# Local attention: the second and third head of every second list swap the engines that evacuate their banks

## The chip, the cores and the metric

The kernel runs on one core of a Trainium2 chip. The metric is the device time of one execution in microseconds (us). A NeuronCore has TensorE (PE in the profile; PEld is its weight load), VectorE (DVE), ScalarE (ACT), GpSimd (POOL) and SyncE (SP), each with an instruction queue of its own, worked off in order; they wait for each other through semaphores. Matmuls write to PSUM banks, of which ScalarE and VectorE bring the results to SBUF.

## The reference, cut to what matters

The program is a two-layer hybrid on an image of 256 channels and 64 x 64 pixels. The change lies in layer 0, a linear attention over boxes around each pixel, with 8 heads of 32 channels and three window sizes:

```python
q = sigmoid(Wq x);  k = sigmoid(Wk x);  v = Wv x / |Wv x|      # x: group-normalised, per head 32 x 64 x 64
Ik, Ikv = integral(k), integral(k outer v)                     # integral images
for w in (1, 2, 4):                                            # boxes of 64, 32 and 16 pixels a side
    attn = einsum('bdhw,bdfhw->bfhw', q, box(Ikv))             # for each pixel: sum of (q.k) v over its box
    norm = einsum('bdhw,bdhw->bhw', q, box(Ik))
    outs.append(attn / (norm + 1e-6))
x = x + Wout(concat(outs)) + bout
```

Layer 1 follows on the 4096 pixels as tokens: causal attention, its feed-forward part, a mixture of experts with two experts chosen, and layer norms. It isn't touched.

## The kernel before

`window_attention` does layer 0 in two head groups of four heads each (`hg` 0 and 1), through `window_heads`. A box sum is split into a part of whole blocks of 8 x 8 pixels, which is taken from block sums (`inside`), and rims. For the rims the kernel forms explicit scores between a tile of 128 keys and a patch of queries, with a mask: a bias of 0 inside the box and -64 outside is added by a matmul with a small table, and a maximum with 0 then wipes what lies outside, since all q and k are positive.

The patches (`Part`) are packed into lists of at most 512 columns, one PSUM bank for each head. In each head group there are 49 vertical lists (`beside`, columns of blocks) and then 108 horizontal ones (`above`, rows of blocks), together 157; `push` handles one list:

1. it takes four psum buffers, one for each head, from a pool of six (`ps`, `bufs=6`), which are handed out in turn;
2. L351: one bias matmul for each part and head, with the heads innermost; the four heads lie on different rows of the TensorE array (32 partitions each) and run side by side;
3. L360: one score matmul for each part and head, q against the keys, in the same banks;
4. `evacuate` (L326 to L330), once for each head in the order 0, 1, 2, 3: maximum with 0 from PSUM to the tile `pm`, by ScalarE (L328) or by VectorE (L330), as a counter says;
5. `add` of the list before: L393, the products of its `pm` with v (tiles `v` or `vh`), summed in accumulators `acc` from a second PSUM pool of two.

The counter runs on over the lists of a head group and is set to 0 at its start. So the dealing repeats after eight evacuations, which is two lists.

TensorE, GpSimd, VectorE and ScalarE run in the order of the program text in this part (`manual_schedule`). On TensorE that gives: bias and scores of list n, products of list n - 1, bias and scores of list n + 1, and so on. A buffer that a list takes must have been evacuated by the engine that holds it. Since four of six buffers belong to the list before, the new list's first two heads get buffers that have been free for long, its third and fourth those of heads 0 and 1 of the list before. Other steps between the lists take buffers from the same pool and shift this: `norms` (`sum_up` L468, `spread_out` L478), `convolve` (L507) and the first steps of layer 1 (`turn`, L887).

Between the lists VectorE and ScalarE do other work: ScalarE copies finished vertical accumulators out (`store`, L404) and sends them to DRAM; VectorE multiplies or adds finished rows (`finish`, L424, L427), takes reciprocals of the norms in four pieces (`invert`, L473), builds block sums (`inner`, L492 to L500) and adds the output projection to the tokens (L512). GpSimd forms the boxes of k (`boxes`, L443 to L456) and multiplies by the reciprocal norms (L428). The raw image for the second head group is loaded into the pool that also holds `pm` (`load`, L190) and normalised (L612).

Of the kernel before, what the change touches and what calls it, by code (L numbers as in the profile page):

```python
# [296 lines left out]
def window_heads(tc, a, t, ident, hg, norm, raws, load, psum, pools, tables, consts, late, causal):  # L297
# [25 lines left out]
    counter = [0]  # L323

    def evacuate(dst, src):
        counter[0] += 1  # L326
        if counter[0] % 8 in (1, 3, 5, 6, 0):
            nc.scalar.activation(dst, src, AF.Relu)  # L328
        else:
            nc.vector.tensor_scalar_max(dst, src, 0.0)  # L330
# [9 lines left out]
    def push(parts):  # L340
# [25 lines left out]
        for h in range(4):  # L366
            evacuate(pm[:, h, 0:at], got[h][:, 0:at])
# [1150 lines left out]
```

## Time and profile before

| | |
|---|---|
| median of 3 runs | 1851.17 us (1850.91 to 1852.68) |
| the profiled execution | 1852.58 us, span 1850.9 us |
| mean granted TensorE clock | 0.986 of full speed |
| TensorE busy over the span | 1773.5 us (96%) |
| VectorE busy | 1017.3 us (55%) |
| ScalarE busy | 834.2 us (45%) |
| GpSimd busy | 510.7 us (28%) |

How to read it: a busy time is the union of an engine's instructions. TensorE's matmuls are pipelined and their ends are modelled, so that a busy TensorE need not be one that gets on. In a line of the timeline stand the start, the duration, the engine, the source line and the operation of instructions that were merged; "out<-in" names the tiles, "x4" is their number, and the bracket tells how long the engine idled before and what ended that. In a line of groups the last part gives busy time and mean duration in ns, then the idle time before and what ended it. The lists of the change run from 75 to 945 us of the span.

### The profile page before, as it was taken

The numbers are of one execution on the slowest core, as the hardware profiler recorded it, in microseconds if no ns is written. First come the engines' busy times: TensorE is split into PE (matmuls) and PEld (weight loads), VectorE is DVE, ScalarE is ACT, GpSimd is POOL, SyncE is SP. The second block draws the span as 40 slices with busy tenths as digits, with TensorE's granted clock in tenths as the row PEclk, the third lists the DMA queues.
The fourth block names the chain that finished last, engine by engine and source line by source line (L and its number), as shares of the span: only waits on it lengthen the run. The fifth ranks groups of instructions, "written<-read, shape, count | busy, mean of one in ns | idle before, by whom it ended". The sixth has DMA issues, their size and how long they took to land.

```text
span 1850.9 us, 41533 instructions
## 1 busy us (share of the span) xinstructions
PE 1773.5 (96%) x17740; PEld 1203.0 (65%) x17740; DVE 1017.3 (55%) x2068; ACT 834.2 (45%) x1588; POOL 510.7 (28%) x767
## 2 busy tenths in 40 slices
PE   6999999999899999999999999999999999699998
PEld 4654555555465455555568888878778777478777
DVE  6544556666464566677663345554565565634333
ACT  3566444444356655545422334544444544432232
POOL 2484223342147123333212022022012112032110
PEclk9999999999999999999999999999999999799999
DMA  5331100000231110000200000000000000010000
GB/s 179 115 99 59 30 14 19 14 19 13 91 108 42 42 30 14 19 13 18 55 2 1 0 1 1 1 1 1 1 1 1 1 1 1 7 51 12 23 23 23
DMA packets 66617, 53.03 MB, mean 29 GB/s; under 512 B 37312, under 2 KB 56536, under 8 KB 66432
## 3 DMA queue, kind: packets, MB, share of 16 engines
q1 hardware_dynamic: 52688, 27.67, 5.5%
q10 hardware_dynamic: 12480, 18.87, 3.0%
q0 software_dynamic: 1264, 3.84, 0.8%
q8 instruction: 139, 2.28, 0.5%
q14 instruction: 46, 0.38, 0.1%
HBM read 32.93 MB, written 17.44 MB: 27 GB/s over the span
## 4 chain that ended last, share of the span: by engine, by line
PE 44%; DVE 5%; ACT 2%; issue 1%; POOL 0%; ACTq 0%; DVEq 0%; POOLq 0%
PE pa L1042 10%; PE po L1115 10%; PE ph L1452 6%; PE py L1472 6%; PE pm L971 1%; PE pm L1176 1%; PE pm L1185 1%; PE acc L393 1%; PE ps L507 1%; DVE lnst L735 1%; PE ps L360 1%; DVE max L1058 1%; PE pm L899 1%; ACT s L1054 1%; DVE s L1093 1%
## 5 line engine op out<-in xcount | busy, mean ns | idle before, releaser
L328 ACT ACTIVATE pm<-ps 128x448 f32<-128x448 f32 (+12 forms) x784 | 368.5, 534 | 326.3 <-issue 174.1
L330 DVE TENSOR_SCALAR pm<-ps 128x448 f32<-128x448 f32 (+15 forms) x472 | 272.3, 605 | 255.6 <-PE ps L360 161.5
L360 PE MATMUL ps<-q,kh 32*128 32x248 f32 (+14 forms) x2688 | 213.5, 397 | 0.0
L393 PE MATMUL acc<-pm,vh 128*32 128x248 f32 (+14 forms) x2688 | 201.4, 401 | 0.0
L1042 PE MATMUL pa<-qT,k 128*128 128x256 f32 (+1 forms) x800 | 184.9, 375 | 0.0
L1058 DVE TENSOR_TENSOR max<-max,pa 128x512 f32<-128x512 f32 x105 | 71.7, 683 | 189.8 <-ACT s L1054 189.7
L351 PE MATMUL ps<-table,table 32*128 32x192 bf16 (+9 forms) x1984 | 158.3, 284 | 8.5 <-ACT pm L328 5.7
L1094 ACT ACTIVATE s<-s 128x512 f32<-128x512 f32 x136 | 85.5, 630 | 178.5 <-DVE s L1093 174.8
L1042 PEld LDWEIGHTS pa<-qT,k 128*128 128x128 f32 x800 | 150.2, 190 | 23.6 <-issue 2.2
L351 PEld LDWEIGHTS <-table 32*128 32x128 bf16 x1984 | 51.3, 91 | 166.3 <-issue 160.6
L428 POOL TENSOR_TENSOR y<-y,rn 128x512 f32<-128x512 f32 x32 | 41.0, 1281 | 416.6 <-DVE y L427 364.3
L360 PEld LDWEIGHTS ps<-q,kh 32*128 32x128 f32 x2688 | 125.2, 184 | 8.1 <-issue 4.9
L393 PEld LDWEIGHTS acc<-pm,vh 128*32 128x32 f32 x2688 | 64.8, 108 | 90.2 <-issue 72.6
L1054 ACT COPY s<-pa 128x512 f32<-128x512 f32 x120 | 69.9, 582 | 115.1 <-PE pa L1042 115.0
L1472 PE MATMUL py<-w,hT 128*128 128x256 f32 x512 | 111.8, 379 | 0.0
L1115 PE MATMUL po<-kh,s 128*128 128x257 f32 x406 | 105.6, 388 | 2.5 <-ACT s L1094 2.5
L1472 PEld LDWEIGHTS py<-w,hT 128*128 128x128 f32 x512 | 97.3, 190 | 15.7 <-issue 1.9
L360 PE MATMUL ps<-q,k 32*128 32x448 f32 (+5 forms) x1280 | 99.1, 403 | 0.0
L393 PE MATMUL acc<-pm,v 128*32 128x448 f32 (+5 forms) x1280 | 96.4, 409 | 0.0
L1093 DVE TENSOR_TENSOR s<-s,tops 128x512 f32<-128x512 f32 x136 | 95.2, 704 | 1.0 <-ACT tops L1086 1.0
L507 PE MATMUL ps<-l0wo,y 128*128 128x256 f32 x384 | 90.7, 387 | 0.0
L1115 PE MATMUL po<-v,s 128*128 128x257 f32 x342 | 86.9, 385 | 1.8 <-ACT s L1094 1.8
(320 smaller groups left out, 2890.4 us busy)
## 6 DMA issues: line engine op xcount, KB each, us to landing
oscratch<-ov ACTq DMA_DIRECT2D x32, 256.0 KB
ov<-oscratch SPq DMA_DIRECT2D x32, 256.0 KB
vscratch<-v SPq DMA_DIRECT2D x32, 128.0 KB
vh<-vscratch SPq DMA_DIRECT2D x16, 256.0 KB
t<-in_xT ACTq DMA_DIRECT2D x16, 256.0 KB
raw<-in_x ACTq DMA_DIRECT2D x7, 512.0 KB
raw<-in_x SPq DMA_DIRECT2D x7, 512.0 KB
out<-y SPq DMA_DIRECT2D x7, 512.0 KB
```

Of the source, the lines that this page charges most:

```text
L328: nc.scalar.activation(dst, src, AF.Relu)
L330: nc.vector.tensor_scalar_max(dst, src, 0.0)
L351: nc.tensor.matmul(got[h][:, spot].rearrange("p (y x) -> p y x", y=part.r1 - part.r0), lhsT=spread[hs, int(part.vertical), :], rhs=bias[hs ...
L360: nc.tensor.matmul(got[h][:, spot].rearrange("p (y x) -> p y x", y=part.r1 - part.r0), lhsT=keys[hs], rhs=q[hs, part.r0 : part.r1, part.c0 ...
L393: nc.tensor.matmul(out, lhsT=v, rhs=pm[:, h, spot].rearrange("p (y x) -> p y x", y=part.r1 - part.r0), start=fresh, stop=(left[key] == 0), ...
L507: nc.tensor.matmul(pt[:, i * D : (i + 1) * D], lhsT=ys[wi, Y][:, (2 * j + i) * P : (2 * j + i + 1) * P], rhs=wo[:, n, :], start=(n == 0), ...
L1042: nc.tensor.matmul(pp[:, k * 2 * P + at : (k + 1) * 2 * P], lhsT=key, rhs=qT[:, c, q0 + at : q0 + 2 * P], start=(c == 0), stop=(c == DC - 1))
L1058: nc.vector.tensor_tensor(u["max"], old, pp, op=ALU.max)
L1093: nc.vector.tensor_tensor(s, s, u["top"].unsqueeze(1).to_broadcast([P, 2, 2 * P]), op=ALU.subtract)
L1115: nc.tensor.matmul(acc, lhsT=u[b][:, (2 * k + j) * P : (2 * k + j + 1) * P], rhs=v[2 * b + k][:, 0 : D + 1], start=(b == h and k == 0), st ...
L1452: nc.tensor.matmul(ph, lhsT=w1v[:, e, c, f, :], rhs=x2[g][c], start=(c == 0), stop=(c == DC - 1))
L1472: nc.tensor.matmul(py, lhsT=hT[:, e, f, j * P : (j + 1) * P], rhs=w2v[:, e, f, :], start=(e + f == 0), stop=(e == 1 and f == FC - 1))
```

## The change

`evacuate` sends the count modulo 8 to ScalarE where it is in a set, and to VectorE otherwise. One member of the set changes:

```diff
     def evacuate(dst, src):
         counter[0] += 1
-        if counter[0] % 8 in (1, 3, 5, 6, 0):
+        if counter[0] % 8 in (1, 3, 5, 7, 0):
             nc.scalar.activation(dst, src, AF.Relu)
         else:
             nc.vector.tensor_scalar_max(dst, src, 0.0)
```

| | head 0 | head 1 | head 2 | head 3 |
|---|---|---|---|---|
| even lists, before and after | ScalarE | VectorE | ScalarE | VectorE |
| odd lists, before | ScalarE | ScalarE | VectorE | ScalarE |
| odd lists, after | ScalarE | VectorE | ScalarE | ScalarE |

Lists are numbered from 0 in each head group, so 78 of the 157 are odd.

## The prediction

> **What bounds the kernel now.** I read the totals of the page first, then the busy time in four stretches (the two passes over the vertical lists, 75 to 190 and 538 to 652 us, and the two over the horizontal lists, 190 to 476 and 652 to 945 us), then the waits, then the costliest groups, and last the timeline around single lists.
>
> ```profile
> PE 1773.5 (96%) x17740; PEld 1203.0 (65%) x17740; DVE 1017.3 (55%) x2068; ACT 834.2 (45%) x1588; POOL 510.7 (28%) x767
> ```
> ```profile
> 190.00:476.00 286.00, 283.42 (x4572) 154.46 (x4567) 174.03 (x288) 136.39 (x289) 89.12 (x103) 1.00 0.07 17
> 652.00:945.00 293.00, 290.38 (x4619) 159.45 (x4611) 202.62 (x391) 144.78 (x309) 88.61 (x99) 1.00 0.09 22
> ```
> The columns of the stretches are PE, PEld, DVE, ACT and POOL busy, the granted clock, the DMA share and GB/s. TensorE is marked busy 99% of both stretches at full clock; VectorE is busy 61 to 69%, ScalarE about 48%, GpSimd 30%. So TensorE's own queue sets the end of this stage, and only time inside that queue can be won.
>
> ```profile
> PE ps L351 <- ACT pm L328: 5.7, 28, 0.2
> ```
> ```profile
> L328 ACT ACTIVATE pm<-ps 128x448 f32<-128x448 f32 (+12 forms) x784 | 368.5, 534 | 326.3 <-issue 174.1
> L330 DVE TENSOR_SCALAR pm<-ps 128x448 f32<-128x448 f32 (+15 forms) x472 | 272.3, 605 | 255.6 <-PE ps L360 161.5
> ```
> In the waits of the first 1000 us, TensorE is idle for ScalarE's evacuations for 5.7 us only, 28 times. That figure is too small: it counts a gap only where the modelled end of the matmul before has passed. The timeline shows the rest. Here are two lists in a row with one part of the same shape each (448 columns); lines of other engines are left out:
>
> ```profile
> 154.88 1.51 ACT L328 ACTIVATE pm<-ps 128x488 f32<-128x488 f32 x3 [1.27 <-PE ps L360]
> 155.03 0.67 DVE L330 TENSOR_SCALAR pm<-ps 128x488 f32<-128x488 f32 x1 [1.17 <-issue]
> ...
> 155.53 0.79 PE L351 MATMUL ps<-table,table 32*128 32x448 bf16 x4
> ...
> 155.98 1.09 PE L360 MATMUL ps<-q,k 32*128 32x448 f32 x8
> ...
> 157.00 1.03 PE L393 MATMUL acc<-pm,v 128*32 128x168 f32 x16
> 157.08 0.98 ACT L328 ACTIVATE pm<-ps 128x448 f32<-128x448 f32 x2 [0.69 <-ACT pm L328]
> 157.13 1.16 DVE L330 TENSOR_SCALAR pm<-ps 128x448 f32<-128x448 f32 x2 [1.44 <-PE ps L360]
> ...
> 157.97 0.37 PE L351 MATMUL ps<-table,table 32*128 32x448 bf16 x4
> ...
> 158.17 0.92 PE L360 MATMUL ps<-q,k 32*128 32x448 f32 x8
> 159.02 0.96 PE L393 MATMUL acc<-pm,v 128*32 128x448 f32 x8
> ```
> At 155.53 us four bias matmuls, one per head, should start within 0.01 us of each other and run side by side. Instruction by instruction, three do; the fourth starts at 155.98, 0.05 us after ScalarE's second evacuation of the list before ended. From first bias matmul to first product this list takes 157.00 - 155.53 = 1.47 us; the next one, behind a list dealt two and two, takes 159.02 - 157.97 = 1.05 us. TensorE lost 0.42 us and the page called it busy.
>
> **The change part by part.** Six psum buffers serve four heads. List n+1 normally gets the two free buffers and then the banks of heads 0 and 1 of list n, so its third and fourth bias matmuls wait for those two evacuations. In an odd list (0 based) ScalarE now takes heads 0, 1 and 3 and VectorE head 2; afterwards ScalarE takes 0, 2, 3 and VectorE 1. Even lists stay. Nothing is added or removed: ScalarE keeps 784 evacuations, VectorE 472, with the same shapes. In the built order only TensorE's waits differ: at L351, 156 move from ScalarE to VectorE and 46 the other way; at L393, 110 move from VectorE to ScalarE.
>
> What the bank of head 1 gains: over the 156 odd lists ScalarE's second evacuation starts a median 0.44 us after its first and takes 0.54; VectorE's single one starts 0.11 us after ScalarE's first and takes 0.62. VectorE ends a median 0.25 us sooner, though in 19 lists later, where it is busy with something else. The Trainium skill (ScalarE: Activation LUTs, Step-by-step) says "ScalarE is closer to PSUM, VectorE is closer to SBUF"; by that alone a bank handed to VectorE would come free later. The rows agree on the length, 0.62 against 0.54 us, but the bank no longer stands second in a queue, which is worth more.
>
> For the sum I took each list's four bias matmuls one by one, replaced the end of the awaited evacuation by that of the engine that will do it (VectorE's single evacuation and ScalarE's second keep their times and swap banks), and let a matmul start 0.051 us after it, as 191 waits of the trace do. From first to fourth bias matmul, summed:
> - 93 odd lists whose successor takes the banks as above: 24.9 us now, 8.7 afterwards, 16.2 won.
> - 17 whose successor has a ScalarE or VectorE wait further ahead, but where again only the fourth moves: 6.8 now, 3.2 afterwards, 3.6 won.
> - 46 where other work took buffers between (convolve, spread_out, turn), so that the successor needs heads 1 and 2 both: 6.3 us either way; 0.03 won, called nothing.
> The sum is 19.9 us, half in each head group (10.3 and 9.6), over 110 waits.
>
> Does TensorE's queue give this back? Among the one-part 448-column lists (40 of them), a fourth matmul that is 0.01, 0.23 and 0.44 us behind the first gives 1.050, 1.255 and 1.470 us to the first product. Over 18 shapes it is the same: what is lost is the stall less some 0.014 us, since the other three heads absorb that much. So 40 stalls that vanish give back 40 x 0.014 = 0.6 us less. Replaying the stage with every engine's order and durations moves 0.2 us more, where a faster TensorE meets a late VectorE. Net 19.9 - 0.6 - 0.2 = 19.1 us.
>
> The other new waits: products of head 2 now wait for ScalarE's second evacuation, but they start after the next list's scores, one microsecond or so after it. The bank of head 2 comes free 0.25 us later; it goes to the list after next as its first buffer, behind a whole list's products. Behind the fourth bias matmul stands all of TensorE's queue, so a late VectorE costs in full; the two lists where it would (at 324.7 and 751.1 us, 0.06 and 0.24 us later) are in the sum. GpSimd and the DMAs move with TensorE. GpSimd waits 50.8 us in two places for L468 in the vertical passes, so 4.5 us won in each does not bring it onto the path.
>
> The profiled execution took 1852.58 us (span 1850.9), 1.4 above the median of 1851.17. 1852.58 - 19.1 = 1833.5; against the median **1832.1 us**.
>
> **Rivals.**
> - *Only the idle time counts.* If the merged rows are right that TensorE waits 5.7 us, no more than that comes: 1851.2 - 5.7 = 1845.5. Against it stand the pairs of equal lists. 5%.
> - *The stage ends elsewhere.* If GpSimd's boxes or the loads between the head groups set the end, the gain is swallowed: about 1851. For it: TensorE does wait for loads near 476 to 483 us. Against: those loads start when TensorE's products free the buffers, so they move along. 5%.
> - *VectorE late, slower.* The bank of head 1 leaves an engine that always comes at once for one that is 61 to 69% busy. In the horizontal lists VectorE also has 64 reciprocals of 0.94 us (L473) and 31 adds of 0.69 (L427). If those now stood ahead of head 1 in the odd half of the lists, each costs its length less the 0.25 us margin: 32 x 0.69 + 15 x 0.44 = 28.7 us, so 28.7 - 19.1 = 9.6 us slower, 1860.8. It decides where VectorE's start is late by more than 0.25 us on average; today VectorE is the later of the two in 8 of the 110 waits that count, and in six of these TensorE comes later than both. 3%.
> - *The clock falls otherwise.* Behind the stage the granted clock is 0.62 over 10.2 us (from 1574.4) and 0.56 over 20.4 us (from 1608.6). Moved forward by 19 us, TensorE's idle stretches there may meet one such drop more or less; one of the size of the first is 0.38 x 10.2 = 3.9 us: 1836.0, or 1828.2. The Trainium skill (TensorE: Matmul & The Clock Gate, What's actually happening) says that the activity window is free-running, about 3.4 us long, so that the drop depends on where in it the work lands. The windows here are of such lengths, but the three runs of before lie within 1.8 us, so it seldom matters. 7%, half each way.
>
> **How the numbers follow.** My forecast, TensorE passing on nearly all of the 19.1 us, has 80%: 1832.1, give or take 4 for the other engines' interplay. The range 1828 to 1840 holds this case and most of the clock's; the idle-only rival, the swallowed gain and the slower case stay outside, 13% in all. A measurement of this kernel can tell about 0.2%, 3.7 us, from no change. Faster is 80 + 7 + 5 = 92%, same 5%, slower 3%.
>
> **What would show it.** Right: in the changed profile the fourth bias matmul behind odd lists follows VectorE's single evacuation; the L351 waits for L328 fall well below 5.7 us, some waits for L330 appear in their place; the list whose bias matmuls start at 155.53 us takes about 1.24 us to its first product where it took 1.47; the last L393 product of the stage ends some 19 us sooner, half of it in each head group; from there on all stands as before but earlier. Wrong: L351 waiting long for L330 with L473 or L427 ahead of it; a stage that ends as late as before with TensorE idle for L612, L446 or a load; or the stage 19 us shorter and the time behind it longer, at a lower clock.

## The result, and the profile after

| | before | after |
|---|---|---|
| median | 1851.71 us (6 runs, 1850.91 to 1852.80) | 1834.01 us (6 runs, 1832.68 to 1836.38) |
| profiled execution | 1852.58 us, span 1850.9 | 1832.68 us, span 1831.0 |
| span's start to the first L351 | 75.3 us | 73.8 us |
| first to last L351, first head group | 397.9 us | 388.8 us |
| from there to the second head group's first L351 | 65.6 us | 65.8 us |
| first to last L351, second head group | 403.2 us | 393.8 us |
| from there to the end | 909.0 us | 908.7 us |

The ratio is 0.9905, 95% interval 0.9892 to 0.9917: faster by 17.7 us, where 19.1 were forecast and 1832.1 us predicted. The profiled execution of after happens to be the fastest of its six. The last five rows, read from the trace of the profiled execution, say where the time came from: 9.1 and 9.4 us out of the two runs of lists, 18.2 us with what lies between; behind them 0.3 us. The 1.4 us at the start are not the change's: over all the kernels with an unchanged start that point lies between 73.8 and 75.3 us.

The totals of the page after:

```profile
PE 1759.7 (96%) x17740; PEld 1198.3 (65%) x17740; DVE 1008.5 (55%) x2068; ACT 833.9 (46%) x1588; POOL 512.4 (28%) x767
```
The instruction counts are the same, and ScalarE's busy time is within 0.3 us of what it was. TensorE's "busy" time fell by 13.8 us although it executes the same matmuls: most of what was won had been counted as work.

The groups of the page and the waits of TensorE over the first 1000 us, after:

```profile
L328 ACT ACTIVATE pm<-ps 128x448 f32<-128x448 f32 (+12 forms) x784 | 368.5, 535 | 308.7 <-issue 173.9
L330 DVE TENSOR_SCALAR pm<-ps 128x448 f32<-128x448 f32 (+15 forms) x472 | 272.0, 604 | 238.0 <-PE ps L360 151.5
```
```profile
PE ps L351 <- ACT pm L328: 1.3, 4, 0.3
...
PE ps L351 <- DVE pm L330: 0.6, 3, 0.2
```
An evacuation costs what it did (534 and 605 ns before). The idle time for ScalarE went from 5.7 to 1.3 us, and 0.6 us for VectorE appeared. The view shows 3.8 us of change where the stage took 18.2 us less.

The timeline of after around the two equal lists of the prediction (lines of other engines and of weight loads left out):

```profile
152.28 1.51 ACT L328 ACTIVATE pm<-ps 128x488 f32<-128x488 f32 x3 [1.21 <-PE ps L360]
152.38 0.67 DVE L330 TENSOR_SCALAR pm<-ps 128x488 f32<-128x488 f32 x1 [1.08 <-issue]
152.94 0.51 PE L351 MATMUL ps<-table,table 32*128 32x448 bf16 x4
153.14 1.06 PE L360 MATMUL ps<-q,k 32*128 32x448 f32 x8
154.13 1.03 PE L393 MATMUL acc<-pm,v 128*32 128x168 f32 x16
...
155.09 0.37 PE L351 MATMUL ps<-table,table 32*128 32x448 bf16 x4
...
156.14 0.96 PE L393 MATMUL acc<-pm,v 128*32 128x448 f32 x8
```
The three evacuations of ScalarE take 1.51 us as before, VectorE's one 0.67. But the fourth bias matmul now waits only for VectorE, until 152.38 + 0.67 = 153.05 us, and not for ScalarE's second evacuation; instruction by instruction it starts at 153.10. The four are spread over less time (L351 x4 lasts 0.51 us, 0.79 before), and the first product comes 154.13 - 152.94 = 1.19 us after the first bias matmul, where it was 1.47 (1.24 was forecast). The list after it takes 1.05 us as before: nothing was there to be won.

### The profile page after: what moved, and what is told of

Read it like the earlier page. It is cut to its first block, busy times and chain, and to the rows that moved or that the text cites. A ratio compares the mean times of both kernels' runs of the same rounds, so it can differ in the third digit from the quotient of the medians.

```text
span 1831.0 us, 41533 instructions
## 1 busy us (share of the span) xinstructions
PE 1759.7 (96%) x17740; PEld 1198.3 (65%) x17740; DVE 1008.5 (55%) x2068; ACT 833.9 (46%) x1588; POOL 512.4 (28%) x767
## 4 chain that ended last, share of the span: by engine, by line
PE 88%; DVE 6%; ACT 3%; issue 1%; DMA 1%; POOL 1%; ACTq 0%; DVEq 0%; POOLq 0%
PE acc L393 14%; PE ps L360 13%; PE pa L1042 11%; PE po L1115 10%; PE ph L1452 6%; PE py L1472 6%; PE ps L351 6%; PE ps L507 5%; PE ps L519 3%; PE acc L412 2%; PE pm L1176 2%; PE pm L971 2%; PE ps L542 1%; PE pm L1185 1%; PE ps L478 1%
## 5 line engine op out<-in xcount | busy, mean ns | idle before, releaser
L351 PEld LDWEIGHTS <-table 32*128 32x128 bf16 x1984 | 50.4, 91 | 157.8 <-issue 152.8
L351 PE MATMUL ps<-table,table 32*128 32x192 bf16 (+9 forms) x1984 | 144.3, 284 | 3.1 <-ACT pm L328 1.3
```

What stands on the lines that cost most here:

```text
L351: nc.tensor.matmul(got[h][:, spot].rearrange("p (y x) -> p y x", y=part.r1 - part.r0), lhsT=spread[hs, int(part.vertical), :], rhs=bias[hs ...
```

## The experiments

The theory: list by list, TensorE's queue stands at the fourth bias matmul until the bank of head 1 is free; what counts is how soon the first two heads' banks are both free, and each such stall is lost in full. The rivals: only the idle time that the waits view shows can be won; it is the engine (VectorE on head 1) or the sharing out as such that helps; VectorE's other work takes the gain back. Ratios are to the kernel before on the same chip. "Spread" is the time from the first to the fourth first-part bias matmul, summed over lists, and "stage" the time from the first L351 to the last one; both are from the one profiled execution, the ratio from all runs.

### One part of the lists alone

```diff
-        if counter[0] % 8 in (1, 3, 5, 7, 0):
+        if counter[0] % 8 in ((1, 3, 5, 7, 0) if counter[0] <= 196 else (1, 3, 5, 6, 0)):   # vertical_only
+        if counter[0] % 8 in ((1, 3, 5, 6, 0) if counter[0] <= 196 else (1, 3, 5, 7, 0)):   # horizontal_only
```

> The new dealing in the 49 vertical lists of each head group only. Theory (TensorE's fourth bias matmul waits for ScalarE's second evacuation, list by list, and the gains add): the replay of the trace gives 8.4 us less than before in the stage, so a ratio of about 0.9955 (0.9945 to 0.9965). Rival (only the idle time that the waits view shows can be won, 5.7 us over all lists, about half of it here): 0.9985. Rival (all lists are needed, or one part alone carries the gain): 1.000 or 0.990.

> The new dealing in the 108 horizontal lists of each head group only. Theory: 11.3 us less than before, ratio about 0.994 (0.993 to 0.995), so that the two parts together give what the whole change gives. Rival (idle time only): 0.9985. Rival (VectorE's other work, which lies here, takes the gain back): 0.998 or more.

Measured: vertical lists alone 0.9960 (0.9946 to 0.9974), stage 7.6 us shorter (8.4 expected); horizontal lists alone 0.9943 (0.9931 to 0.9955), stage 10.1 us shorter (11.3 expected). 7.6 + 10.1 = 17.7 us, against 18.2 for both. The stretch between the two head groups, which is part of the stage, runs from 63.2 to 67.4 us over the thirteen profiles, so a stage figure is good to some 2 us; the runs of lists alone are 7.2 us shorter in vertical_only and 12.0 in horizontal_only. The gain is local and adds up; VectorE's reciprocals and adds in the horizontal lists do not take it back. The idle-only rival gave 0.9985 for each and falls with both: the intervals end at 0.9974 and 0.9955.

### Which engine takes which head

```diff
-        if counter[0] % 8 in (1, 3, 5, 7, 0):
+        if counter[0] % 8 in (1, 3, 6, 7, 0):      # mirrored: odd lists VectorE, ScalarE, ScalarE, ScalarE
+        if counter[0] % 8 in (1, 3, 5, 6, 7):      # vector_last: odd lists ScalarE, ScalarE, ScalarE, VectorE
```

> In odd lists VectorE takes head 0 and ScalarE heads 1, 2 and 3; even lists as they were. Theory (the first two heads' banks must come free in parallel, whichever engine takes which): 19.7 us less in the stage by the replay, as for the change itself, ratio 0.990 to 0.992. Rival (it is VectorE on head 1, or ScalarE on head 0, that matters): between 0.995 and 1.002.

> In odd lists ScalarE takes heads 0, 1 and 2 and VectorE head 3. Theory (head 1 stands second in ScalarE's queue as before, and head 2 now third): no gain; where the successor needs heads 1 and 2 it waits longer, 3.3 us more in the stage by the replay, ratio 1.001 to 1.003. Rival (another sharing out, with ScalarE's three in a row ending no later, is what helped): 0.990 to 0.995.

Measured: mirrored 0.9902 (0.9888 to 0.9917), the same as the change, stage 20.3 us shorter. So it is not VectorE on head 1 that helps: VectorE on head 0 does as well. vector_last 0.9991 (0.9982 to 0.9999), where 1.001 to 1.003 was expected. The interval excludes that range, if by little. The spread behind odd lists did not move (37.8 us, 38.0 before) and the two runs of lists are 1.1 us longer together than before; the stage is 1.3 us shorter only because the load between the head groups took 2.3 us less. Another sharing out gains nothing in the lists, as the theory says. The 3.3 us of loss that I expected did not come: the 46 lists behind which other work took buffers waited 0.3 us less, not more.

### The suspected cost made larger

```diff
-        if counter[0] % 8 in (1, 3, 5, 6, 0):      # the kernel before
+        if counter[0] % 8 in (1, 2, 5, 6, 0):      # even lists too: ScalarE heads 0 and 1
```

> The suspected cost made larger: ScalarE takes heads 0 and 1 of every list, even lists too (VectorE heads 2 and 3 there; in odd lists as before). Each engine keeps its number of evacuations. Theory: the fourth bias matmul now waits for ScalarE's second evacuation behind even lists too; by the replay 18.5 us more than before in the stage, ratio 1.008 to 1.012. Rival (only idle time, as the waits view counts it): some 5.7 us more, 1.003. Rival (sharing out does not matter as long as the counts are the same): 1.000.

Measured: 1.0072 (1.0058 to 1.0085), stage 15.0 us longer. The spread behind even lists rose by 19.2 us (11.6 to 30.8), that behind odd lists fell by 4.0. The sign and the order of size are the theory's, and the interval excludes both rivals' 1.003 and 1.000; the 18.5 us of the replay were too many, and the ratio lies below the 1.008 to 1.012 that were expected. Of the 4.0 us, 3.9 fell on the 110 odd lists whose successor takes the banks of heads 0 and 1: there ScalarE's second evacuation ends a mean 0.12 us after the successor's first bias matmul, 0.16 before. Why it ends sooner there is open. The waits of TensorE over the first 1000 us in this kernel:

```profile
PE ps L351 <- ACT pm L328: 5.7, 29, 0.2
```
5.7 us, to the digit what the kernel before shows with 28 waits, in a kernel whose stage takes 15.0 us more. The view does not show the stalls that were added; as at 155.53 us in the kernel before, a gap does not count where the modelled end of the bias matmul ahead covers it.

### What the faster TensorE ran into

In the 158 lists that come first in a head group or behind an even list, whose dealing did not change (the "other" lists), the spread rose from 11.6 to 13.4 us in the changed kernel. It rose most at four vertical lists of the first head group. The timeline of after at one of them (lines of other engines and of weight loads left out):

```profile
110.82 0.92 PE L360 MATMUL ps<-q,k 32*128 32x448 f32 x8
111.02 0.61 ACT L404 COPY ov<-acc 128x512 f32<-128x512 f32 x1
111.66 0.35 ACTq L405 DMA_DIRECT2D oscratch<-ov  x1
111.67 0.96 PE L393 MATMUL acc<-pm,v 128*32 128x448 f32 x8
111.87 1.16 DVE L330 TENSOR_SCALAR pm<-ps 128x448 f32<-128x448 f32 x2 [1.46 <-PE ps L360]
112.03 0.46 ACTq L658 DMA_DIRECT2D t<-in_xT  x1
112.56 0.31 PE L351 MATMUL ps<-table,table 32*128 32x320 bf16 x2
112.59 0.98 ACT L328 ACTIVATE pm<-ps 128x448 f32<-128x448 f32 x2 [0.96 <-DVE pm L330]
113.19 0.31 PE L351 MATMUL ps<-table,table 32*128 32x320 bf16 x4 [0.32 <-ACT pm L328]
```
The scores end near 111.7 us and VectorE starts at 111.87. ScalarE copies an accumulator, issues its store and then a load of t, and starts on head 0 at 112.59. TensorE starts two bias matmuls at 112.56 and the next only at 113.19, 0.6 us later. Three kernels take the issues from ScalarE (mirrored_sp has the mirrored dealing besides):

```diff
-                    nc.scalar.dma_start(out=t[:, i : i + 2, :], ...)      # L658
+                    nc.sync.dma_start(out=t[:, i : i + 2, :], ...)        # after_xt, after_sp, mirrored_sp
-        nc.scalar.dma_start(out=oscratch[wi][X], in_=o)                   # L405
+        nc.sync.dma_start(out=oscratch[wi][X], in_=o)                     # after_sp, mirrored_sp
```

> The changed kernel with the loads of t (L658, 16 issues in the first head group's vertical lists) issued by SyncE instead of ScalarE. Theory (behind four of the even lists there ScalarE comes late, since it issues two DMAs of 0.35 and 0.46 us after the copy of L404, and the change let TensorE come earlier without ScalarE): those lists lose up to 0.5 us less each, some 1 to 2 us less than the changed kernel, ratio to before 0.9895 against 0.9905. Rival (those issues fill idle time of ScalarE): no difference to the changed kernel.

> As after_xt, and the 32 stores of L405 issued by SyncE too. Theory: ScalarE has neither issue before the next list, in both head groups; 2 to 4 us less than the changed kernel, ratio to before 0.988 to 0.9895. Rival: no difference, or SyncE's queue, which also carries the loads of L683, makes the horizontal lists wait and gives it back.

> As after_sp, with the mirrored dealing (VectorE head 0, ScalarE heads 1, 2, 3 in odd lists). The mirrored stage took 2.1 us less than that of the changed kernel in the profile; if the two add, ratio to before 0.987 to 0.989; if the mirrored gain was scatter, as after_sp.

Measured: 0.9920 (0.9906 to 0.9933), 0.9912 (0.9898 to 0.9925) and 0.9908 (0.9893 to 0.9923): not better than the change. The first head group's lists did get shorter, 385.9, 385.7 and 385.1 us against 388.8, but the first L351 came at 80.2 to 81.0 us instead of 73.8. From the first 30 us, the wait of L200 in the changed kernel and in after_xt, and SyncE's loads of t in after_xt:

```profile
ACT L200 <- issue: 13.6, 1, 13.6
```
```profile
ACT L200 <- DMA t<-in_L_Wk: 18.6, 1, 18.6
```
```profile
5.82 15.87 SPq L658 DMA_DIRECT2D t<-in_xT  x9
```
The edit moved the loads in time as well. ScalarE issued the 16 loads from 80.9 to 144.2 us; on SyncE nothing ties them to the lists, and they go out from 5.8 to 49.0 us, at the start of the program (the row shows the first nine). The mean busy share of the DMA engines over the first 30 us rises from 0.67 to 0.90. They also alternate with ScalarE's early loads in taking the eight semaphores on which loads are counted, so that several of these wait for another load than before: the sixth (L777) is issued at 18.2 us instead of 13.1, and L200, behind it in ScalarE's queue, starts 5 us late. What the order of the waits and what the added traffic cost, the runs do not separate.

So the next edit (apart, and mirrored_apart with the mirrored dealing) leaves the loads with ScalarE, but issues none after a list that finished an accumulator:

```diff
                 push(parts)
-                if hg == 0 and i % 2 == 0 and i < NT:
+                calm = not any(key[0] and left[key] == 0 for key in {part.key for part in lists[i]})
+                if hg == 0 and calm and at2[0] < NT:
+                    n = at2[0]; at2[0] += 2
                     nc.scalar.dma_start(out=t[:, n : n + 2, :], ...)
```

> The changed kernel as it is, on the same chip as the next two, so that they can be compared with it. Ratio to before 0.9905, as found first.

> The changed kernel, with the 16 loads of t (L658) still issued by ScalarE but only after lists in which no vertical accumulator was finished, so that the copy L404, its store L405 and a load never stand in a row ahead of ScalarE's next evacuation. With the loads on SyncE the first head group's lists took 3.0 us less, but the kernel's start 6.5 us more, as the order of the early DMAs changed with it; here it stays. Theory (a late ScalarE behind even lists cost that): 1 to 3 us less than the changed kernel, ratio to before 0.9885 to 0.990. Rival (the 3.0 us came from the later start of the stage, not from the issues): no difference.

> As apart, with the mirrored dealing. If mirrored is worth what its profile showed (2.1 us of the stage), 2 us less than apart, ratio to before 0.987 to 0.989; otherwise as apart.

Measured: the change again 0.9900 (0.9883 to 0.9916), apart 0.9892 (0.9876 to 0.9909), mirrored_apart 0.9897 (0.9880 to 0.9913). In the profile the first L351 of apart is at 74.8 us again, the first head group's lists take 385.6 us against 388.8, the second's are unchanged (394.0 against 393.8; the change, profiled twice, took 388.8 and 393.8 both times), and the spread behind the other lists is back at 11.6 us. So the shorter lists do not hang on a later start of the stage, as the rival had it. The same place in apart:

```profile
111.26 0.34 ACTq L405 DMA_DIRECT2D oscratch<-ov  x1
111.27 0.96 PE L393 MATMUL acc<-pm,v 128*32 128x448 f32 x8
111.47 1.16 DVE L330 TENSOR_SCALAR pm<-ps 128x448 f32<-128x448 f32 x2 [1.46 <-PE ps L360]
111.71 0.54 ACT L328 ACTIVATE pm<-ps 128x448 f32<-128x448 f32 x1 [0.48 <-PE ps L360]
111.75 0.37 ACTq L662 DMA_DIRECT2D t<-in_xT  x1
112.15 0.54 ACT L328 ACTIVATE pm<-ps 128x448 f32<-128x448 f32 x1
112.16 0.45 PE L351 MATMUL ps<-table,table 32*128 32x320 bf16 x6
```
The load now goes out behind the start of the first evacuation, ScalarE starts 0.44 us after the products (111.27) where it was 0.92, and TensorE's fourth bias matmul comes 0.14 us after its first where it was 0.63. The stage is 2.7 us shorter than in changed_again. The medians, 1831.97 against 1833.88 us, go the same way, but their intervals overlap: that apart beats the change is shown in the first head group's lists and only likely in the whole time. The mirrored dealing adds nothing: its stage is 846.0 us, that of apart 846.1.

## Why the prediction was right, point by point

- *What bounds the stage.* Right. Both head groups ended sooner by what TensorE's queue no longer stood still, and everything behind them kept its length.
- *The sum over the lists.* Behind the 93 odd lists of the plain kind 17.6 us were won (16.2 predicted), behind the 17 others 4.2 (3.6), behind the 46 with heads 1 and 2 both needed 0.0 (0.03). The surplus comes from VectorE: it now starts a median 0.07 us after ScalarE's first evacuation, 0.11 before, and ends 0.29 us ahead of ScalarE's second, 0.25 before. That shift was not in the sum.
- *The even lists.* Here the prediction fell short. They were called unchanged, and put at 0.2 us for VectorE in the replay. They cost 1.8 us, 1.0 of it in eight vertical lists (four in each head group) where ScalarE came late behind a copy and its DMA issues; the replay had left the time of such issues out. ScalarE is thus not "an engine that always comes at once". Over all lists the surplus and this loss cancel, which is luck: the spread fell by 20.0 us, predicted 19.9.
- *The give-back.* Some 54 stalls vanished, not 40; at 0.014 us each that gives back 0.8 us, not 0.6. Another 0.8 us went at one place near the start of the lists (between the second and the third list), and 0.2 between the head groups. 20.0 - 0.8 - 0.8 - 0.2 = 18.2 us, the stage's gain. The forecast's 1832.1 us lies 1.9 below the measured median: 0.9 is the stage (19.1 against 18.2), 0.5 the median of before, which stands at 1851.71 with six runs, and the other 0.5 is less than the scatter of the runs.
- *The rivals.* Only the idle time: fell, most plainly by both_scalar. The stage ends elsewhere: fell by the table. VectorE late: it was late where foreseen (the list at 751.1 us before, 734.6 after: spread 0.20 to 0.44 us), in two or three lists, not on average. The clock: it did not come in. Behind the stage both profiles have the same six drops to 0.50 of full clock, 45.4 us in all, and the time there differs by 0.3 us. The prediction's window for the first long drop lay 2.5 us too late: the drop reaches from 1571.9 to 1582.1 us at 0.50, so by the prediction's own working it is worth 0.50 x 10.2 = 5.1 us, not 3.9. The chance for this rival was not for nothing: over the thirteen profiles the drops behind the stage sum to 38.9 to 48.6 us and the time there runs from 906.9 us (both_scalar) to 911.1 (mirrored_apart). Each of these drops lasts 3.4, 10.2 or 20.5 us, but for the last, which the end of the span cuts. The Trainium skill (TensorE: Matmul & The Clock Gate, What's actually happening) gives a window of 3.4 us; the lengths agree, being one, three and six times that, and whether the window is free-running no run here shows.
- *The engine nearer to PSUM.* With mirrored as good as the change, the placement that the Trainium skill names (ScalarE: Activation LUTs, Step-by-step) decides nothing that shows here: VectorE's 604 ns against ScalarE's 535 matter less than standing second in a queue.

## What to carry to other kernels

When a ring of PSUM buffers feeds back into the matmul queue, find which buffers the next group takes first, and have exactly those evacuated first and by different engines; the counts per engine say nothing about that (they are the same in the change, at 0.9905, and in both_scalar, at 1.0072). Do not read the price off an idle column when an engine's ends are modelled: compare the start times of equal pieces of work with and without the wait. And a queue that evacuates should not issue DMAs just ahead of the evacuation that is awaited; here that was worth some 3 us in the first head group.

## What the runs showed that I had not expected

- The idle column stayed at 5.7 us while the same wait grew by 15.0 us of stage time (both_scalar).
- ScalarE's DMA issues of 0.35 and 0.46 us, with a copy ahead of them, cost TensorE 0.4 to 0.5 us in each of four lists before the change and about 0.6 after it.
- Sixteen loads that were only to change queues also moved from the vertical lists to the start of the program, and the first bias matmul came 5 to 7 us later.
